# Layer 0's aggregation turned: weighted features stationary in 32-column groups, masked p moving, own waves for the denominators

## The chip, the cores and the metric

The kernel runs on one core of one Trainium2 chip. A core has a matrix engine (TensorE, PE in the profile, with its weight loads as PEld), a vector engine (VectorE, DVE), a scalar engine (ScalarE, ACT), a general engine (GpSimd, POOL) and an engine that here only starts transfers (SyncE, SP). Matrix products land in PSUM, eight banks of 128 partitions by 512 fp32 numbers; everything else works from on-chip memory. A product has a stationary operand, which is loaded as weights (up to 128 columns), and a moving operand that is streamed past it (up to 512 columns).

The metric is the device time of one execution in microseconds.

## The reference, cut to what matters

Thirty-two graphs of 512 nodes with 256 features go through four layers, each with a residual: a graph attention with 4 heads of 64 features (layer 0), one with one head and softmax over the other axis (1), one with scores from the features themselves (2), and a transformer block with 8 heads and a feed-forward part (3). The change is in layer 0:

```python
h = maximum(layernorm(x), 0)
Wh = (h @ W).reshape(B, N, H, F)                      # H = 4, F = 64
e_src = einsum('bnhf,hf->bnh', Wh, a_src)
e_dst = einsum('bjhf,hf->bjh', Wh, a_dst)
e = leaky_relu(e_src[:, :, None, :] + e_dst[:, None, :, :], 0.2)
e = where((A > 0)[..., None], e, -1e9)
alpha = softmax(e, axis=2)
Hout = elu(einsum('bijh,bjhf->bihf', alpha, Wh))
x = x + Hout.reshape(B, N, H * F)
```

For node i and head h, the sum over neighbours j of exp(e) times the features of j is wanted, and the sum of exp(e) itself, the denominator, to divide by.

## The kernel before, in words

All work is recorded first and put in order afterwards. `layer0` to `layer3` (lines 804 to 1061) call helpers of a `Plan`: `plan.dve`, `plan.act`, `plan.dma`, `plan.matmuls` (lines 220 to 273). Each call becomes a job of one engine. A job's place in the order is a number from a written list: `PLACES` (line 291) for the graphs in the middle and `OWN` (line 334) for the first three and the last three, one number per job in the order of recording, plus 100000 per graph. `carry_out` (line 179) sorts all jobs by place and issues them so; within an engine the order is fixed. The durations given in the calls (such as 0.867) were for whoever made the lists and do not act at run time. Because all instructions are issued from these helpers, the profile names lines 215, 236, 266 and 268 for nearly all of them, and one goes by the names of tiles. Four graphs are under way at a time: while layer 0 of graph b runs, so do layer 1 of b-1, layer 2 of b-2 and layer 3 of earlier ones. `WARM` (line 591) lists places at which products with no use are put in to keep TensorE going.

Tiles come from a few kinds of buffers (lines 623 to 633). `half` has 8 slots of 128x512 that `p`, `y`, `to` and `inv` share. `ps` has 8 slots, one for each PSUM bank. A job that needs a slot waits until the slot's last user is done.

Layer 0 of one graph: the normalised rows h are transposed and multiplied with the weights (`ps_wh`). With leaky ReLU of slope 0.2, exp(e_src + e_dst) is, up to a factor that the division by the denominator takes away, max of two products, so a tile of p needs one VectorE instruction: for head hd and block j of 128 source nodes, `p` = max(rows[hd], a column of rt) times the mask, 128 source nodes by 512 target nodes. `rows` has the target side's values spread over all partitions: a small transpose (`ps_sp`), a store to DRAM and a broadcast load (`spread`, line 750). `wh[:, j, hd]` has the 64 features of block j for head hd, weighted, and their weight as a 65th column, so one product gives both sums.

The aggregation before: head by head, four p tiles, then for each of four target blocks i four products that add up over j, each with a 128x128 piece of p stationary and the 65 columns of `wh` moving. The result for a head lies in one bank with target nodes on partitions; VectorE takes the reciprocal of column 64 and multiplies.

Layer 3 already has a step of the form that the change brings to layer 0. Its context product `ps_ct` has 32 columns of `v` stationary and p moving, four heads in one call, each in its own 32 partitions of the bank; `ps_to` sums the denominators in the same way with a block of ones. The chain behind `ps_to` is: copy to on-chip memory (`to`), a store and a load that reorder it (`seen`), a reciprocal (`turned`), a store and a broadcast load (`inv`), and the multiplication of `cT`. Then come the output projection `ps_wo`, a normalisation to `n`, its transposition to `tT` and the feed-forward products `ps_f`.

Of the kernel before, what the change touches and what calls it, by code (L numbers as in the profile page):

```python
# [19 lines left out]
P = 128  # L20
# [255 lines left out]
def cut(i, n):  # L276
    return slice(i * n, (i + 1) * n)
# [6 lines left out]
def width(args):  # L284
# [7 lines left out]
    22162, 0, 22162, 88531, 22162, 26725, 27163, 44460, 126207, 331647, 206240, 126207, 317201, 18267, 20761,  # L292
    18708, 20761, 20761, 20761, 19602, 20856, 20856, 20856, 21830, 21830, 21830, 22732, 23337, 26934, 26317,
    22732, 26696, 27107, 27107, 30449, 53386, 34079, 34079, 38928, 51388, 52104, 54992, 57816, 58763, 57816,
    60568, 60081, 64657, 58365, 58866, 58866, 60717, 59413, 60717, 69440, 61691, 69039, 58515, 59806, 61012,
    69310, 73463, 76565, 74335, 77480, 55624, 59714, 61810, 60113, 66193, 63085, 62613, 62147, 61810, 61828,
    66013, 71581, 76689, 73222, 74340, 71581, 80778, 81737, 82695, 84674, 95332, 99599, 91796, 94089, 94085,
    93641, 99780, 99871, 99871, 99871, 104897, 111173, 100627, 103661, 102330, 106673, 110040, 110040, 110439,
    110702, 110702, 111173, 103192, 98821, 100354, 103331, 104973, 109811, 109811, 114440, 115166, 117019,
    120459, 121784, 121784, 139316, 133372, 142407, 137472, 142753, 142177, 142576, 137500, 142780, 142780,  # L300
    142996, 142996, 145490, 146534, 182835, 158676, 172770, 165625, 182835, 182835, 184170, 184170, 185322,
    184815, 184929, 184929, 184929, 187876, 187397, 200306, 200306, 185322, 188856, 198107, 188211, 188638,
    192607, 197637, 197826, 198409, 201283, 201244, 200306, 208481, 210062, 211700, 211941, 233602, 234284,
    235911, 235911, 211941, 217912, 218005, 241001, 224079, 224079, 230987, 230987, 236039, 237560, 237560,
    241953, 245593, 248489, 249477, 249813, 250667, 250344, 253110, 255044, 255044, 255614, 260717, 250695,
    250667, 257382, 257239, 257910, 257011, 257816, 257582, 257910, 258536, 259626, 259626, 260717, 260717,
    262805, 263575, 263165, 265205, 264400, 265625, 266248, 266260, 266977, 265939, 265939, 265939, 266047,
    266654, 268571, 268656, 269410, 270114, 271651, 274286, 274286, 280210, 280492, 283576, 283576, 275998,
    270461, 272338, 272338, 272770, 275869, 283576, 283576, 283576, 292056, 279418, 280186, 281828, 287241,
    293813, 295621, 299513, 293813, 280342, 280342, 285316, 280607, 292528, 292528, 285495, 301515, 301515,  # L310
    293861, 309042, 323663, 299920, 310909, 323056, 302045, 313927, 315695, 324108, 326725, 328805, 333540,
    335674, 330312, 335674, 333540, 335674, 335674, 335674, 335674, 335674, 335674, 337792, 335674, 335945,
    337538, 337792, 338472, 338472, 339430, 338064, 338995, 339085, 339805, 339430, 341861, 340079, 342248,
    342386, 343136, 363657, 365495, 365712, 343496, 344786, 346786, 361418, 362306, 363732, 360543, 361672,
    363606, 363615, 364988, 366453, 366470, 366470, 367867, 371472, 350129, 350129, 351023, 351522, 350129,
    352607, 373487, 352053, 355399, 354213, 353318, 352495, 358682, 375835, 360752, 354916, 357414, 356045,
    356979, 356501, 363165, 376453, 365438, 357934, 359672, 361968, 358915, 359382, 367305, 376453, 367305,
    373487, 376011, 376011, 376214, 377681, 379922, 386609, 386609, 391610, 368361, 371551, 370334, 369094,
    370632, 372872, 389527, 372949, 376689, 376689, 376689, 375390, 376689, 389527, 379922, 378070, 379951,
    378381, 379951, 379951, 379951, 389752, 386116, 378530, 386611, 381015, 386341, 380335, 386655, 392660,  # L320
    386655, 391743, 393582, 393733, 397668, 393911, 397668, 398447, 399849, 404727, 406119, 396110, 408587,
    408587, 408587, 408587, 408532, 408672, 408672, 408672, 408672, 408833, 408587, 408672, 408672, 408901,
    409041, 408843, 408851, 409041, 409165, 409165, 409165, 409165, 409165, 409200, 409200, 412312, 412594,
    410533, 411146, 413463, 414091, 413863, 414031, 414685, 414779, 414604, 414779, 425712, 432774, 417564,
    417600, 418973, 414994, 418406, 418406, 417704, 420814, 423607, 416056, 423251, 424719, 419148, 419463,
    426062, 419047, 425810, 426096, 422579, 426020, 427996, 426052, 426052, 426481, 427471, 427663, 427663,
    428663, 428815, 428815, 428815, 428815, 428815, 428815, 428815, 436411, 441991, 442166, 442166, 442334,
    442892, 426062, 426062, 426062, 426062, 426062, 426120, 428517, 429214, 429626, 429626, 431772, 432297,
    432526, 438547, 440425, 440425, 440425, 445487, 442892, 445367, 445261, 445606, 444750, 445596, 445914,
    445914, 446041, 447300, 447300, 447822, 447822, 448286, 447822, 447822, 447822, 449213, 454171, 455710,  # L330
    501496, 619074, 561825,
# [4 lines left out]
        0, 0, 0, 119376, 103, 103, 103, 849, 849, 135780, 267957, 849, 12430, 0, 0, 0, 0, 0, 0, 0, 0, 0, 0, 0, 0, 0,  # L336
        0, 0, 0, 0, 0, 0, 0, 0, 0, 0, 0, 0, 0, 0, 0, 11, 11, 11, 11, 24105, 2715, 1981, 1981, 0, 11, 11, 12, 8848,
        13263, 12, 994, 0, 698, 698, 720, 24151, 18142, 11140, 30522, 698, 698, 698, 698, 698, 19312, 7058, 5132,
        698, 769, 769, 907, 12093, 907, 2071, 10598, 24151, 24151, 24427, 24427, 26204, 26204, 20723, 22597, 24775,
        17243, 24775, 24775, 24775, 26442, 29386, 30515, 24834, 27433, 27101, 27305, 27636, 28305, 28305, 28305,  # L340
        36756, 38640, 33391, 33391, 33391, 32763, 33391, 34992, 37365, 37365, 39631, 39631, 39631, 41962, 41990,
        44686, 43031, 46645, 46952, 48602, 50627, 50627, 50627, 50627, 52044, 52287, 52287, 52287, 54403, 57069,
        59970, 67793, 68704, 57330, 72067, 72067, 76307, 76307, 57069, 70179, 70179, 76449, 87103, 90440, 91113,
        91113, 86657, 91775, 91830, 89730, 89730, 89830, 84870, 88104, 88104, 91830, 95736, 146060, 95736, 110896,
        110896, 111056, 151052, 162807, 171370, 193307, 144090, 146060, 161198, 161281, 169706, 177493, 178851,
        193307, 159830, 168071, 175630, 192102, 193307, 194008, 203693, 203960, 204523, 208395, 211891, 211891,
        211891, 211891, 541, 206953, 207979, 217639, 217841, 208042, 220030, 219958, 222074, 223137, 223137, 223268,
        223695, 223695, 223695, 223695, 223962, 224666, 227528, 223695, 226442, 226476, 227561, 228090, 225042,
        226400, 226400, 227561, 227561, 229120, 243465, 241449, 251907, 251907, 251968, 261633, 261633, 261633,
        262685, 268778, 267860, 241176, 253160, 264725, 254084, 264725, 265569, 271684, 271711, 268778, 251945,  # L350
        258419, 272733, 270637, 272733, 281556, 281556, 274321, 266409, 266409, 272414, 268107, 274733, 275414,
        276199, 281751, 281751, 283148, 283148, 283148, 286088, 286088, 286088, 283645, 283645, 283645, 285852,
        283148, 286088, 283645, 285852, 283829, 286088, 287226, 287226, 287247, 287247, 287247, 290195, 290195,
        290195, 290324, 290324, 290927, 290324, 290324, 290324, 291288, 290195, 290380, 290783, 297351, 291438,
        311506, 407069, 309785, 314007, 314007, 352851, 353546, 353546, 320788, 320788, 320788, 328304, 334485,
        339755, 350640, 350991, 351191, 356570, 356636, 360260, 360260, 360260, 364578, 368069, 323179, 323676,
        323723, 323613, 323610, 356339, 367007, 324585, 327970, 329761, 330936, 330730, 345176, 372128, 358994,
# [231 lines left out]
}  # L589

WARM = [
    (1906, 1), (21908, 1), (24150, 2), (44209, 4), (45938, 1), (223694, 9),
]

def quick_path(
# [38 lines left out]
    def new(tag, name, shape, dtype=F32):  # L636
        return plan.tile(K[tag], name, shape, dtype)
# [958 lines left out]
```

## Time and profile before

| | us |
|---|---|
| median of 3 runs | 3472.92 |
| lowest and highest | 3470.82, 3476.01 |
| the profiled execution | 3479.19 |
| its span on the core | 3477.2 |
| TensorE busy | 3399.2 |
| VectorE busy | 2840.4 |
| ScalarE busy | 2082.5 |

The granted TensorE clock over the span was 0.993 of full speed. A row of the groups view names line and engine, the operation, the tiles written and read, the shapes and the count, then busy time and mean duration of one, then how long the engine stood idle before it and what ended that. A matrix product of fp32 operands appears as two passes with a weight load each; a transpose is one pass. Passes overlap in the pipeline, so a mean duration is longer than the distance from one start to the next; the rows in order of time give that distance.

### The profile page before, as it was taken

How to read it: one execution, taken by the hardware profiler on the slowest of the kernel's cores; microseconds unless marked ns; L12 is line 12 of the kernel's file. 1: busy time of each engine (PE TensorE's matmuls, PEld its weight loads, DVE VectorE, ACT ScalarE, POOL GpSimd, SP SyncE). 2: the span in 40 equal slices, each digit the busy share in tenths (PEclk: the TensorE clock that was granted, in tenths of full speed). 3: DMA queues.
4: the chain of work that ended last, by engine and by line, in shares of the span. 5: the costliest groups of instructions: out<-in, count | busy, mean ns of one | idle time of the engine just before them, and what ended most of it. 6: DMA issues, size and time to landing. Idle time of an engine off the chain costs nothing.

```text
span 3477.2 us, 49596 instructions
## 1 busy us (share of the span) xinstructions
PE 3399.2 (98%) x18474; PEld 2310.3 (66%) x18474; DVE 2840.4 (82%) x5659; ACT 2082.5 (60%) x4705; POOL 11.1 (0%) x25
## 2 busy tenths in 40 slices
PE   6999999999999999999999999999999999999996
PEld 5766766766666766666666666667667666667554
DVE  5888888888888788888888887888888888877874
ACT  4656566556576556675566665566665565764652
POOL 1000000000000000000000000000000000000000
PEclk9999999999999999999999999999999999999998
DMA  5111111111111111111111111111111120110000
GB/s 161 43 52 54 36 43 53 44 50 56 32 47 52 38 56 50 38 45 54 38 56 50 35 46 52 41 56 38 41 52 44 50 68 32 40 47 20 13 8 26
DMA packets 161176, 161.23 MB, mean 46 GB/s; under 512 B 92576, under 2 KB 126880, under 8 KB 156832
## 3 DMA queue, kind: packets, MB, share of 16 engines
q1 hardware_dynamic: 158464, 153.00, 14.8%
q0 software_dynamic: 1216, 3.94, 0.3%
q8 instruction: 147, 2.41, 0.3%
q10 hardware_dynamic: 1248, 1.05, 0.1%
q14 instruction: 101, 0.83, 0.1%
HBM read 122.96 MB, written 18.22 MB: 41 GB/s over the span
## 4 chain that ended last, share of the span: by engine, by line
PE 86%; DVE 7%; DMA 3%; ACT 2%; issue 1%; DVEq 0%; SPq 0%
PE ps_f L268 25%; PE ps_o L268 22%; PE ps_s L268 6%; PE ps_wh L268 6%; PE ps_ct L268 6%; PE ps_qk L268 5%; PE ps_t L266 4%; PE ps_e L268 4%; PE ps_wo L268 3%; DVE p L215 3%; PE ps_v L268 2%; DMA inv<-in_d 2%; DVE acc L215 2%; PE ps_to L268 1%; DVE st L215 1%
## 5 line engine op out<-in xcount | busy, mean ns | idle before, releaser
L268 PEld LDWEIGHTS ps_o<-wh,p 128*128 128x128 f32 x5120 | 673.1, 192 | 86.6 <-issue 55.0
L268 PE MATMUL ps_o<-wh,p 128*128 128x65 f32 (+1 forms) x5120 | 723.5, 295 | 0.4 <-DVE o L215 0.4
L215 ACT ACTIVATE p<-ps_s 128x512 f32<-128x512 f32 x1024 | 563.0, 625 | 59.9 <-PE ps_s L268 55.1
L215 DVE TENSOR_TENSOR p<-p,m 128x2048 f32<-128x2048 f32 x256 | 582.8, 2278 | 12.2 <-ACT p L215 12.0
L268 PE MATMUL ps_f<-ff_t,f 128*128 128x256 f32 x2048 | 476.4, 380 | 0.0
L268 PE MATMUL ps_f<-tT,ff_t 128*128 128x512 f32 x1024 | 454.4, 599 | 0.7 <-ACT tT L215 0.7
L268 PEld LDWEIGHTS ps_f<-ff_t,f 128*128 128x128 f32 x2048 | 377.9, 190 | 81.2 <-issue 34.0
L215 DVE SCALAR_TENSOR_TENSOR p<-rows,seen,mT 128x512 f32<-128x512 f32 x512 | 364.8, 740 | 14.6 <-PE ps_o L268 11.9
L268 PEld LDWEIGHTS ps_f<-tT,ff_t 128*128 128x128 f32 x1024 | 192.7, 191 | 229.8 <-issue 208.2
L215 ACT ACTIVATE h<-x,shift,rstd 128x256 f32<-128x256 f32 x512 | 299.2, 636 | 54.5 <-DVE shift L215 54.5
L215 ACT ACTIVATE rstd<-mv,eps 128x4 f32<-128x4 f32 x192 | 56.9, 297 | 446.8 <-DVE mv L215 262.0
L215 DVE TENSOR_TENSOR acc<-acc,p 128x2048 f32<-128x2048 f32 x128 | 292.9, 2288 | 3.2
L268 PE MATMUL ps_s<-qk 32*128 32x512 f32 x2048 | 287.6, 633 | 0.8 <-ACT qk L215 0.8
L268 PE MATMUL ps_qk<-h3T,wqkv_t 128*128 128x512 f32 x512 | 249.0, 594 | 1.2 <-ACT p L215 1.2
L268 PE MATMUL ps_o<-h,p 128*128 128x257 f32 x1024 | 246.7, 384 | 0.0
L268 PE MATMUL ps_ct<-p,v 128*32 128x512 f32 x2048 | 244.7, 595 | 1.4 <-ACT v L215 1.4
L215 ACT ACTIVATE f<-ps_f,ff1b_c 128x512 f32<-128x512 f32 x256 | 163.1, 682 | 125.9 <-PE ps_f L268 125.8
L268 PEld LDWEIGHTS ps_o<-h,p 128*128 128x128 f32 x1024 | 189.6, 190 | 47.1 <-PE ps_to L268 20.1
L266 PE MATMUL ps_t<-ident,h 128*128 128x128 f32 x1024 | 173.7, 278 | 29.2 <-ACT h L215 27.4
L215 DVE BATCH_NORM_STATS2 st<-x 128x6 f32<-128x256 f32 x512 | 196.5, 413 | 2.5 <-DMA x<-in_x_dram 0.6
L215 ACT COPY wh<-ps_wh 128x258 f32<-128x258 f32 x128 | 47.8, 377 | 239.5 <-PE ps_wh L268 236.7
L266 PEld LDWEIGHTS ps_t<-ident,h 128*128 128x128 f32 x1024 | 127.4, 144 | 82.7 <-issue 46.9
(126 smaller groups left out, 4600.9 us busy)
## 6 DMA issues: line engine op xcount, KB each, us to landing
adj<-in_adj_dram SPq DMA_DIRECT2D x32, 1024.0 KB
rows<-rows_d SPq DMA_DIRECT2D x32, 1024.0 KB
x<-in_x_dram SPq DMA_DIRECT2D x32, 512.0 KB
rows<-rows_d SPq DMA_DIRECT2D x32, 512.0 KB
inv<-in_d SPq DMA_DIRECT2D x64, 256.0 KB
out_dram<-y SPq DMA_DIRECT2D x32, 512.0 KB
mT<-m SPq DMA_TRANSPOSE x128
ff_t<-in_L_gnn_W_dram POOLq DMA_DIRECT2D x2, 1024.0 KB, 10.5
```

The costliest lines, as they stand in the source:

```text
L215: return [getattr(unit, method)(*map(real, args), **{k: real(v) for k, v in kw.items()})]
L266: made.append(self.nc.tensor.transpose(*map(real, c)))
L268: made.append(self.nc.tensor.matmul(*map(real, c[:3]), start=c[3], stop=c[4]))
```

## The change

The products of layer 0's aggregation are turned around. The stationary operand is now 32 columns of the weighted features, and the moving operand is a whole p tile of 512 target nodes. Two heads with two halves of 32 features each fill the four 32-column groups of the array, and their sums the four 32-partition groups of one bank; two such banks (`ps_oT`) hold the 256 features. A third bank (`ps_den`) holds the denominators: per head the weight column, repeated 32 times, is stationary. All three add up over the four source blocks, so the loop now goes over j outside and heads inside. At the end the sums have features on partitions: ScalarE copies each bank to a `half` tile (`oT`), four transposes each bring it back (`ps_or`), and VectorE takes one reciprocal for all heads and multiplies two heads at a time. The lists `PLACES`, `OWN` and `WARM` are new throughout, so the order of all other work is changed too; only `WARM` is shown.

```diff
 WARM = [
-    (1906, 1), (21908, 1), (24150, 2), (44209, 4), (45938, 1), (223694, 9),
+    (6839, 2), (6909, 5), (32585, 1), (47866, 3), (152849, 1), (210837, 9), (342049, 1),
 ]
...
         inv = rt[:, 2 * H0 :]
-        for hd in range(H0):
+        pairs, half = H0 // 2, F0 // 2
+        ps_oT = [new("ps", "ps_oT", [P, N]) for _ in range(pairs)]
+        ps_den = new("ps", "ps_den", [P, N])
+        for j in range(NT):
             ps_t = []
-            for j in range(NT):
+            for hd in range(H0):
                 p = new("p", "p0", [P, N])
                 plan.dve(
                     "scalar_tensor_tensor", p, rows[:, hd], rt[:, H0 + hd, j : j + 1], mT[:, j], OP.max, OP.mult,
                     fixed=0.21,
                 )
                 ps_t.append(p)
-            ps = new("ps", "ps_o", [P, NT, F0 + 1])
+            for g in range(pairs):
+                plan.matmuls(
+                    0.882,
+                    *(
+                        (
+                            ps_oT[g][cut(q, half)], wh[:, j, 2 * g + q // 2, cut(q % 2, half)], ps_t[2 * g + q // 2],
+                            j == 0, j == NT - 1,
+                        )
+                        for q in range(4)
+                    ),
+                )
+            plan.matmuls(
+                0.882,
+                *(
+                    (
+                        ps_den[cut(hd, half)], wh[:, j, hd, F0 : F0 + 1].flat(lambda t: t.to_broadcast([P, half])),
+                        ps_t[hd], j == 0, j == NT - 1,
+                    )
+                    for hd in range(H0)
+                ),
+            )
+        turned = []
+        for ps in (ps_den, *ps_oT):
+            t = new("half", "oT", [P, N])
+            plan.act("copy", t, ps)
+            ps = new("ps", "ps_or", [P, NT, P])
             for i in range(NT):
-                plan.matmuls(
-                    0.867,
-                    *((ps[:, i], ps_t[j][:, cut(i, P)], wh[:, j, hd], j == 0, j == NT - 1) for j in range(NT)),
-                )
-            plan.dve("reciprocal", inv[:, hd], ps[:, :, F0], each=7.5e-3, fixed=0.13)
+                plan.matmuls(0.11, (ps[:, i], t[:, cut(i, P)], ident))
+            turned.append(ps)
+        plan.dve(
+            "reciprocal", inv.flat(lambda t: t.rearrange("p h t -> p t h")),
+            turned[0][:, :, 0:P:half], each=7.5e-3, fixed=0.13,
+        )
+        for g in range(pairs):
             plan.dve(
-                "tensor_mul", o[:, :, cut(hd, F0)], ps[:, :, :F0],
-                inv[:, hd].flat(lambda t: t.unsqueeze(2).to_broadcast([P, NT, F0])),
+                "tensor_mul", o[:, :, cut(g, P)].split("p t (h f) -> p t h f", (NT, 2, F0), h=2),
+                turned[1 + g].split("p t (h f) -> p t h f", (NT, 2, F0), h=2),
+                inv[:, 2 * g : 2 * g + 2].flat(
+                    lambda t: t.rearrange("p h t -> p t h").unsqueeze(3).to_broadcast([P, NT, 2, F0])
+                ),
             )
```

## The prediction

> **What bounds the kernel now.** I read the engine rows of the page first, then the chain, then the groups by form, and last the order of time on TensorE inside one graph of the steady middle.
>
> ```profile
> PE 3399.2 (98%) x18474; PEld 2310.3 (66%) x18474; DVE 2840.4 (82%) x5659; ACT 2082.5 (60%) x4705; POOL 11.1 (0%) x25
> ...
> PEclk9999999999999999999999999999999999999998
> ...
> PE 86%; DVE 7%; DMA 3%; ACT 2%; issue 1%; DVEq 0%; SPq 0%
> ```
>
> TensorE works 98% of the span at full clock and is 86% of the chain that ended last. A busy PE row need not be a PE at its peak, so what one product costs has to be read from start to start. Groups by form (busy us and mean ns, then idle before):
>
> ```profile
> L268 PEld LDWEIGHTS ps_o<-wh,p 128*128 128x128 f32 x5120 | 673.1, 192 | 86.6 <-issue 55.0 <-ACT wh L215 1.1 <-DVE y L215 0.8
> L268 PE MATMUL ps_o<-wh,p 128*128 128x65 f32 x4096 | 481.8, 273 | 0.0
> L268 PE MATMUL ps_ct<-p,v 128*32 128x512 f32 x2048 | 244.7, 595 | 1.4 <-ACT v L215 1.4
> L215 ACT COPY cT<-ps_ct 128x512 f32<-128x512 f32 x64 | 37.3, 587 | 16.8 <-PE ps_ct L268 16.7
> L215 DVE RECIPROCAL seen<-ps_o 128x4 f32<-128x4 f32 x128 | 22.0, 172 | 49.5 <-PE ps_o L268 49.3
> ```
>
> The second row is what the change takes out: 2048 products, two passes each, moving only 65 columns against 128 stationary ones. The third row, layer 3's context product, already has the new form: 32 stationary columns, 512 moving, four such products side by side (a wave of eight passes). Order of time on TensorE in one graph, and around one lone wave earlier on (start, length, x passes):
>
> ```profile
> 1774.51 1.91 PE L268 MATMUL ps_wh<-w_t,h1T 128*128 128x258 f32 x8
> 1776.34 2.78 PE L268 MATMUL ps_ct<-p,v 128*32 128x512 f32 x24
> 1778.94 1.04 PE L268 MATMUL ps_to<-acc,ones 128*32 128x512 f32 x8
> 1779.80 1.04 PE L268 MATMUL ps_ct<-p,v 128*32 128x512 f32 x8
> 1780.77 2.01 PE L268 MATMUL ps_o<-h,p 128*128 128x257 f32 x8
> ...
> 1784.03 3.68 PE L268 MATMUL ps_o<-wh,p 128*128 128x65 f32 x32
> 1787.55 1.96 PE L268 MATMUL ps_o<-h,p 128*128 128x257 f32 x8
> ...
> 1792.46 3.19 PE L268 MATMUL ps_wo<-wo_t,cT 128*128 128x256 f32 x14
> 1795.49 0.78 PE L268 MATMUL ps_o<-wh,p 128*128 128x65 f32 x6
> ```
> ```profile
> 387.47 1.06 PE L268 MATMUL ps_to<-acc,ones 128*32 128x512 f32 x8
> 388.47 1.14 PE L268 MATMUL ps_s<-qk 32*128 32x512 f32 x8
> ```
>
> There are no gaps: each line starts as the one before releases the array. A 65-column pass takes (1787.55-1784.03)/32 = 0.110 us, more than a quarter of what a 512-column one takes. Five waves in a row take 1780.77-1776.34 = 4.43 us and a lone one 1.00, so a further wave costs (4.43-1.00)/4 = 0.857. Entering and leaving the four-column mode costs 1.00-0.857 = 0.14 inside the run, and 0.10 on the product ahead of it: eight passes of ps_wh take 1.83 where 0.216 each (14 passes of ps_wo in 3.03) make 1.73. So 0.24 us per run of waves.
>
> **The change on TensorE.** It is the engine that sets the end, so every term counts in full.
> - Out: 4096 passes x 0.110 = 450.6.
> - In: per graph 4 source tiles x 3 waves (two of weighted features, one of denominators) = 12, times 32 = 384 waves x 0.857 = 329.1.
> - In: 3 x 4 transposes per graph, 384. Seven transposes start at 1751.57 and the next product at 1752.33, so 0.109 each: 41.9.
> - In: mode changes. In the planned order of the two programs, column-mode runs rise from 75 to 138, because most of the new waves stand in two runs of six per graph: 63 x 0.24 = 15.1. Row-mode runs (ps_s) go from 223 to 221, nothing.
> - In: warming products 18 to 22, eight passes more: 1.7.
>
> In is 387.8, out 450.6: **-62.8 us** with no new wait.
>
> Two features of the new waves the trace does not show. Two column groups of a weighted-feature wave stream the *same* p tile, where layer 3's four stream four tiles; and the denominator's stationary columns are one column repeated. Between the free end (0.857, as ps_ct) and full serialisation of the pair (two turns, 1.71, on 256 waves: +219), I take the ps_ct row, as it is the same shape from the same kind of memory. A repeated column can at most make its weight load longer; loads lie under the 0.43 us of the pass before.
>
> Here the Trainium skill speaks against the change. "TensorE: Matmul & The Clock Gate", Part 3, gives 2.38 for three column tiles, not 3; at the same 79% four tiles would give 3.17, and a wave, 4 x 0.857 unpacked (512 columns, two passes of 0.43), would be 1.08 us: 384 x 0.22 = 86 more, and the change would lose 23. "TensorEngine Tiling (Array Packing)", Key Properties, adds that changing the mode drains the array. The trace has both at their price here: 0.857 per wave, 0.24 per run. I sum with the rows.
>
> **The change elsewhere.** VectorE loses 128 reciprocals x 0.172 and 128 products of 256 x 0.413 (74.9 us) and gains 32 reciprocals of 16 x 0.247 and 64 products of 512 x 0.686 (51.8): 0.7 us less per graph. The 16 masked p tiles per graph stay. ScalarE gains 96 copies of 128x512 at 0.587: 56 us, 1.8 per graph, on an engine that is busy 64.9 of the 104.7 us that a graph takes in the middle of the run (from 1747.90 to 1852.60, one row spread of layer 0 to the next). These are covered by TensorE's work except at two places.
>
> (1) *Feed-forward entry.* The out-projection's sums go through VectorE's statistics, four normalisations and tT on ScalarE before ps_f may start. In the graph above ps_wo ends at 1795.49 and ps_f starts at 1802.53: 7.04 us, covered by 65-column products and transposes. After, the planned order covers it with a six-wave run (5.38), eight transposes of n (0.87) and eight of the turned sums (0.87): 7.1, just enough. But two of the new copies (1.17 us) stand on ScalarE's queue between n and tT; what is late next is tT, then ps_f. ScalarE waited 0.42 for its transposes at that point, so up to 0.75 is exposed, down to nothing where the copies fit into such holes.
>
> (2) *The second cT.* VectorE's queue from layer 3's first mask product to this multiplication is full. The trace has it so:
>
> ```profile
> 1787.75 2.75 DVE L215 SCALAR_TENSOR_TENSOR p<-rows,seen,mT 128x512 f32<-128x512 f32 x4 [0.27 <-PE ps_o L268]
> 1791.60 0.69 DVE L215 TENSOR_TENSOR cT<-cT,inv 128x512 f32<-128x512 f32 x1 [1.10 <-DMA inv<-in_d]
> ```
>
> cT ends at 1792.29 and ps_wo starts at 1792.46: no slack already. Summing the rows' durations along VectorE's queue to that point gives 56.0 us in both orders (14 p tiles now stand ahead of it, 12 before, against small work moved out), and TensorE's order gives 57 us in both. So the wait stays as it is, within some 0.5 per graph. Each wave also needs four heads of one source tile; eight p tiles feed a six-wave run and the pool of that size holds eight, shared with y, to and inv. p tiles cost 0.74 each, 3.0 per three waves of 2.57: they must be ahead when a run begins, and the other products between the two runs (some 5 us) let them be.
>
> On SP the number of transfers is unchanged; the layer-0 rows load now follows the first inv load instead of preceding the pair, and has some 9 us before its first use, as 7.5 passed in the trace from its issue at 1750.37 to the first p at 1757.90. I price it at nothing; late rows would delay the first run of waves one for one.
>
> I take 0.45 us per graph for (1) and (2) together, over 29 graphs (the first three fill the pipeline): +13. Sum: -62.8 + 13 = **-50**. The profiled execution took 3479.2 (span 3477.2), which becomes 3429; the median of the runs, 3472.9, becomes **3423**.
>
> **Rivals.**
> - *All covered* (chance 0.15). Waits stay as they are; 3472.9-62.8 = 3410, and about 3395 if the 78 us in which TensorE is not busy (3477.2-3399.2, nearly all in the first and last slices of the page) shrink as well. For it: steady graphs idle little. Against: the copies ahead of tT.
> - *Evacuation and VectorE set the pace* (0.17). Three sums stay in PSUM from the first wave to the last and leave together, ScalarE copies before tT, and a late cT adds to it: 1.5 to 2 us per graph, 44 to 58 of the 62.8 come back: 3454 to 3468, at the worst end no change. For it: VectorE busy 57.94 of the 60 us from 1735 to 1795. Against: the queue sums of (2) are equal.
> - *The waves are dearer than ps_ct's* (0.08), the slower side. If the two groups that stream one p tile take turns, up to +219: 3473-50+219 = 3642. It decides from 50/384 = 0.13 us per wave. For it: no row has that form. Against: four streams run side by side in ps_ct at no cost over one.
> - *The order is not kept in runs*, or array time per graph is otherwise as before (0.02): 3473.
>
> **How the numbers follow.** The case of the sum has 0.58, with its own range 3408 to 3445. A measurement of this kernel tells 0.2% (7 us) from no change: the runs span 5 us. Faster: 0.58 + 0.15 + 0.13 of the pace rival = 0.86. Same: 0.03 of it + 0.02 = 0.05. Slower: 0.08 + 0.01 = 0.09. The range reaches from part of the covered case, 3394, to most of the pace rival, 3460.
>
> **What would show it.** ps_oT and ps_den passes, 3072 in all, with runs of six waves taking 0.14 + 6 x 0.857 = 5.28 us; 384 ps_or passes at 0.109; a steady graph, 104.7 now, at about 103.1; VectorE busy 20 lower, ScalarE 56 higher. Step (1) shows as idle time of ps_or or ps_f waiting for oT or tT. The prediction is wrong if a wave takes over 0.98 us, or if ps_wo or the first wave of a run waits over 1 us per graph.

## The result, and the profile after

The changed kernel takes 3427.1 us (median of four runs, 3424.9 to 3429.9) against 3473.7 for the kernel before on the same chip: a ratio of 0.9867, 95% interval 0.9850 to 0.9884. The forecast was 3423, in a range of 3394 to 3460. Its profiled execution took 3424.9, with a span of 3422.9.

The engine rows, the granted clock and the chain that ended last, from the page of the changed kernel:

```profile
PE 3340.2 (98%) x17842; PEld 1975.5 (58%) x17842; DVE 2820.1 (82%) x5499; ACT 2115.6 (62%) x4801; POOL 11.1 (0%) x25
...
PEclk9999999999999999999999999999999999999997
...
PE 85%; DVE 8%; DMA 4%; ACT 3%; issue 1%; DVEq 0%; SPq 0%; ACTq 0%
```

TensorE's busy time fell by 59.0 us, from 3399.2, and the time in which it isn't busy rose from 3477.2-3399.2 = 78.0 to 3422.9-3340.2 = 82.7: together the 54.3 us by which the two spans differ. (The medians differ by 46.6, since the profiled execution of before lay 5.5 above its median and that of after 2.2 below.) The groups by form (busy us and mean ns, then idle time before and what ended it):

```profile
L268 PE MATMUL ps_ct<-p,v 128*32 128x512 f32 x2048 | 247.8, 599 | 0.0
...
L268 PE MATMUL ps_oT<-p,wh 128*32 128x512 f32 x2048 | 240.6, 594 | 0.0
...
L268 PE MATMUL ps_den<-p,wh 128*32 128x512 f32 x1024 | 129.5, 597 | 0.0
...
L268 PEld LDWEIGHTS ps_oT<-p,wh 128*32 128x32 f32 x2048 | 64.3, 110 | 142.4 <-issue 128.3 <-DVE st L215 8.3 <-DVE p L215 2.3
...
L266 PE MATMUL ps_or<-ident,oT 128*128 128x128 f32 x384 | 62.4, 273 | 0.1
...
L215 ACT COPY oT<-ps_oT 128x512 f32<-128x512 f32 x64 | 37.0, 580 | 14.0 <-PE ps_oT L268 14.0
...
L215 DVE RECIPROCAL seen<-ps_or 128x16 f32<-128x16 f32 x32 | 8.0, 251 | 5.5 <-PE ps_or L266 5.5
```

The 3072 passes of `ps_oT` and `ps_den` take what those of `ps_ct` take (594 and 597 ns against 599, overlapped), a weight load of 32 columns is 110 ns long where that of 128 was 192, and the 384 transposes hardly wait. The repeated column of the denominators costs nothing at its load either: 110 ns at the median, as for the others. One reciprocal of 16 per partition and graph takes the place of four. Order of time on TensorE in a graph of the steady middle (start, length, x passes, and in brackets the wait):

```profile
1635.38 1.06 PE L268 MATMUL ps_to<-acc,ones 128*32 128x512 f32 x8
...
1642.33 1.06 PE L268 MATMUL ps_den<-p,wh 128*32 128x512 f32 x8
1643.21 2.76 PE L268 MATMUL ps_oT<-p,wh 128*32 128x512 f32 x24
1645.79 1.06 PE L268 MATMUL ps_den<-p,wh 128*32 128x512 f32 x8
1646.67 1.04 PE L268 MATMUL ps_oT<-p,wh 128*32 128x512 f32 x8
1647.64 2.00 PE L268 MATMUL ps_o<-h,p 128*128 128x257 f32 x8
1649.49 0.59 PE L268 MATMUL ps_wo<-wo_t,cT 128*128 128x256 f32 x2
1650.64 2.86 PE L268 MATMUL ps_wo<-wo_t,cT 128*128 128x256 f32 x12 [0.56 <-DVE cT L215]
1653.43 3.64 PE L268 MATMUL ps_oT<-p,wh 128*32 128x512 f32 x32
1656.89 1.90 PE L268 MATMUL ps_den<-p,wh 128*32 128x512 f32 x16
1658.72 1.13 PE L266 MATMUL ps_t<-ident,n 128*128 128x128 f32 x8
1659.68 1.04 PE L266 MATMUL ps_or<-ident,oT 128*128 128x128 f32 x8
...
1660.70 1.98 PE L268 MATMUL ps_f<-tT,ff_t 128*128 128x512 f32 x4
```

The second run of six waves lasts from 1653.43 to 1658.72, 5.29 us; the forecast had 5.28. The first, 1642.33 to 1647.64, takes 5.31. A wave that streams one p tile into two column groups, and one whose weights are a single column repeated, cost what `ps_ct`'s cost: 5.29 less the 0.14 at the start is 0.858 for each of six. In this stretch TensorE waits once, 0.56 us for the second cT.

Over the 23 graphs between the row spreads of graphs 5 and 28, start to start, a graph takes 103.41 us (105.29 before). The 64 narrow products took 14.1 us of it before; the twelve waves take 10.6 and the twelve transposes 1.3. The order of all other work is new as well, and the old form in a newly made order was not run. But in these 23 graphs TensorE stood idle for 8.9 us in all before and for 5.4 after, so a better order alone had little to win there.

### The profile page after: what moved, and what is told of

It reads as the page before. It is cut to its first block, busy times and chain, and to the rows that moved or that the text cites. A ratio compares the mean times of both kernels' runs of the same rounds, so it can differ in the third digit from the quotient of the medians.

```text
span 3422.9 us, 48320 instructions
## 1 busy us (share of the span) xinstructions
PE 3340.2 (98%) x17842; PEld 1975.5 (58%) x17842; DVE 2820.1 (82%) x5499; ACT 2115.6 (62%) x4801; POOL 11.1 (0%) x25
## 4 chain that ended last, share of the span: by engine, by line
PE 85%; DVE 8%; DMA 4%; ACT 3%; issue 1%; DVEq 0%; SPq 0%; ACTq 0%
PE ps_f L268 25%; PE ps_o L268 11%; PE ps_s L268 7%; PE ps_qk L268 6%; PE ps_wh L268 5%; PE ps_ct L268 5%; PE ps_oT L268 5%; PE ps_t L266 4%; PE ps_e L268 4%; PE ps_wo L268 3%; DVE p L215 3%; PE ps_v L268 3%; PE ps_den L268 3%; DMA inv<-in_d 2%; DVE acc L215 2%; PE ps_to L268 1%
## 5 line engine op out<-in xcount | busy, mean ns | idle before, releaser
L215 ACT ACTIVATE p<-ps_s 128x512 f32<-128x512 f32 x1024 | 555.3, 616 | 35.0 <-PE ps_s L268 33.7
L268 PE MATMUL ps_f<-tT,ff_t 128*128 128x512 f32 x1024 | 467.1, 597 | 0.4 <-ACT tT L215 0.4
L215 DVE SCALAR_TENSOR_TENSOR p<-rows,seen,mT 128x512 f32<-128x512 f32 x512 | 352.7, 744 | 32.6 <-PE ps_oT L268 20.6
L215 ACT ACTIVATE h<-x,shift,rstd 128x256 f32<-128x256 f32 x512 | 283.1, 599 | 94.5 <-DVE shift L215 94.2
L268 PEld LDWEIGHTS ps_f<-tT,ff_t 128*128 128x128 f32 x1024 | 185.4, 191 | 196.2 <-issue 154.5
L268 PE MATMUL ps_o<-wh,p 128*128 128x256 f32 x1024 | 242.9, 385 | 0.4 <-ACT wh L215 0.4
L268 PE MATMUL ps_oT<-p,wh 128*32 128x512 f32 x2048 | 240.6, 594 | 0.0
L268 PE MATMUL ps_qk<-h3T,wqkv_t 128*128 128x512 f32 x512 | 239.2, 599 | 0.0
L268 PEld LDWEIGHTS ps_o<-wh,p 128*128 128x128 f32 x1024 | 189.9, 190 | 77.0 <-issue 25.9
## 6 DMA issues: line engine op xcount, KB each, us to landing
ff_t<-in_L_gnn_W_dram POOLq DMA_DIRECT2D x2, 1024.0 KB, 10.3
```

The costliest lines, as they stand in the source:

```text
L215: return [getattr(unit, method)(*map(real, args), **{k: real(v) for k, v in kw.items()})]
L268: made.append(self.nc.tensor.matmul(*map(real, c[:3]), start=c[3], stop=c[4]))
```

## The experiments

All times are medians beside the 3427.1 of the changed kernel, which was timed with the result alone; the kernel before took 3472.8 to 3475.3 beside the experiments and 3473.7 beside the changed kernel, so differences of 2 or 3 us say nothing. "Per graph" is the mean over the same 23 graphs, and a product's share of it is counted from each pass's start to the next one's. The letters in the expectations, in short: A, TensorE's list alone sets the end; B, the new order is needed for the gain; C, VectorE sets the pace; D, a change of the array's mode costs less than priced; E, a product's price goes with its moving columns; F, TensorE's and VectorE's lists are equally long; G, a chain of waits runs beside TensorE's list.

**The new form in the old order.** The turned products stand where the old ones stood, with the tables of before; a job is put off only where no buffer is free.

```diff
-PLACES = [ ... ]                      # of after
+PLACES = turned_places(PLACES)        # of before: p tiles and waves at the old places,
+OWN = {n: turned_places(t) for n, t in OWN.items()}   # copies, transposes, products after the last wave
...
-        for number, j in enumerate(sorted(self.jobs, key=lambda j: j.place)):
+        for number, j in enumerate(self.in_turn()):
```

> The turned aggregation in the written order of the kernel before: the new products, copies and transposes stand at the places of the old ones, and a job is put off only where no buffer is free; all other work keeps its place. Theory A (the array time of the aggregation is the gain, whatever the order): TensorE's list loses 450.6 us of 65-column passes and gains 384 waves x 0.857 = 329.1, 384 transposes x 0.109 = 41.9 and, as the waves now stand in 201 runs instead of 138, (201-75) x 0.24 = 30.2: -49, so 3425, and up to 3440 with waits for copies that nothing hides. Theory B (the new written order brings the gain, the form alone does not): 3465 or more.

Measured: 3683.5 us (3681.3 to 3686.6), ratio to before 1.0609 [1.0591, 1.0627]. A graph takes 112.7 us. The products' own time is about 102 of it, as in the changed kernel, but waits make up some 10 us (TensorE is idle for 6.5 by the profile), against about 1.5 in the kernels before and after. TensorE's waits in this kernel (who for whom on which engine: us in total, times, longest):

```profile
PE ps_wh L307 <- DVE p L254: 48.5, 25, 3.0
PE ps_t L305 <- DVE p L254: 47.1, 52, 1.4
...
PE ps_f L307 <- ACT tT L254: 21.4, 32, 1.5
PE ps_wo L307 <- DVE t L254: 18.8, 24, 0.8
```

The products of the first two rows don't read p. The view of the tile `ps_y` (layer 2's transposes) tells what they wait for; among those who waited for an instruction that uses it are (us, times):

```profile
  PE ps_wh L307: 48.5, 25
  PE ps_t L305: 47.1, 52
```

These are the same waits: each ends when VectorE has read `ps_y` out of its PSUM bank into a tile p, so the product waits for a bank. Of the eight banks three are now held from the first wave of a graph to the last, where the old form held one per head. In the changed kernel neither waits for `ps_y`. That the banks make up the whole of the waits wasn't measured. The form alone doesn't bring the gain; it needs an order that fits it. One placement was tried, which needn't be the best.

**Fewer waves.** One denominator wave per graph in place of four.

```diff
+            if j:
+                plan.at += 1
+                continue
             plan.matmuls(0.882, ... ps_den ...
-                        ps_t[hd], j == 0, j == NT - 1,
+                        ps_t[hd], True, True,
```

> The kernel after with the denominator waves of three of the four source blocks left out (so the denominators are partial): 96 waves fewer, all other engines unchanged. Theory A (TensorE still bounds every graph): 96 x 0.857 = 82 less than the kernel after, 3345. Theory C (VectorE's queue of p tiles and masks sets the pace once TensorE is faster): half or less of it, 3385 or more.

Measured: 3432.0 (3427.5 to 3435.9). 96 waves are gone, 82 us of TensorE's list, and nothing is gained: a graph takes 103.90. The same stretch of this kernel, in order of time on TensorE:

```profile
1650.47 2.86 PE L268 MATMUL ps_wo<-wo_t,cT 128*128 128x256 f32 x12 [1.77 <-DVE cT L215]
1653.26 3.64 PE L268 MATMUL ps_oT<-p,wh 128*32 128x512 f32 x32
1657.93 0.82 PE L266 MATMUL ps_t<-ident,n 128*128 128x128 f32 x3 [1.03 <-ACT n L215]
1658.91 0.76 PE L266 MATMUL ps_t<-ident,n 128*128 128x128 f32 x5 [0.16 <-ACT n L215]
```

What was work has become waiting: for cT, which needs the attention's denominators back from DRAM, and for n, the layer norm behind it. The chain that ended last is 70% TensorE here (85% in the changed kernel), with VectorE 17% and DMA 6%.

**More waves.** Each denominator wave is done twice.

```diff
+                    for turn in (0, 1)
                     for hd in range(H0)
```

> The kernel after with every denominator wave issued twice (the denominators are doubled): 128 waves more, nothing else. Theories A and F: each wave lies on TensorE's path, 128 x 0.857 = +110 on the kernel after, 3537, and per graph 103.35 becomes 106.8. A smaller step, under +70, would mean that TensorE has hidden slack.

Measured: 3521.5 (3518.6 to 3524.9), 94 more for 128 waves: 0.74 each, and 106.54 per graph, 3.13 more for four waves (0.78 each). The four waves themselves take 3.46 us from start to start, 0.86 each; `ps_wo` takes 0.31 less, as part of the new work replaces its wait for cT. So TensorE's list does set the end, and has no room to shrink below it: up costs nearly in full, down gives nothing.

**More changes of the mode.** A full-array transpose stands ahead of the first source block's waves, into the same bank.

```diff
+                    *([(ps_oT[g][:, :P], ident, ident)] if j == 0 else []),
```

> The kernel after with one plain full-array transposition ahead of each of the three waves of a graph's first source block (96 in all; what they write is overwritten by the wave). Runs of waves rise from 138 to 199. Theory A (entering and leaving the four-column mode costs 0.24 us): 96 x 0.109 + 61 x 0.24 = +25, so 3452. Theory D (the mode change costs nothing, only the transpositions count): +10, 3437.

Measured: 3445.2 (3442.4 to 3448.3), 18 more, between the two theories (25 and 10); per graph 0.72 more. Three transposes are 0.33 of that, so two further runs cost 0.39, 0.20 each. On TensorE of this kernel:

```profile
1649.49 0.27 PE L266 MATMUL ps_den<-ident 128*128 128x128 f32 x1
1649.69 1.07 PE L268 MATMUL ps_den<-p,wh 128*32 128x512 f32 x8
1650.69 0.33 PE L266 MATMUL ps_oT<-ident 128*128 128x128 f32 x1
1650.95 1.07 PE L268 MATMUL ps_oT<-p,wh 128*32 128x512 f32 x8
1651.94 0.33 PE L266 MATMUL ps_oT<-ident 128*128 128x128 f32 x1
```

A transpose and a lone wave take 1.20 and 1.25 us here; less 0.109 and 0.857, the change of mode costs 0.23 and 0.28, as the forecast's 0.24. The graph pays less because `ps_wo` takes 0.21 less in this kernel: again work replaces its wait for cT.

**The old form with half the columns.** The kernel before, with 33 moving columns in place of 65, so that half of the features are left out.

```diff
-(ps[:, i], ps_t[j][:, cut(i, P)], wh[:, j, hd], j == 0, j == NT - 1)
+(ps[:, i, 32:], ps_t[j][:, cut(i, P)], wh[:, j, hd, 32:], j == 0, j == NT - 1)
```

> The kernel before with 33 instead of 65 moving columns in layer 0's aggregation (half of the features are left out, and the other half stands in their place). Theory A (such a pass is bound by loading its 128 stationary columns): a pass stays at 0.110 us and the time at 3474 within 7. Theory E (it is bound by what it streams): passes fall to 0.06 us or less, 4096 x 0.05 = 205 less, about 3270.

Measured: 3628.3 (3616.6 to 3633.9), ratio 1.0446. The median pass still takes 0.112 us, start to start, so the price of the old form was not in its moving columns. What both have in common is a load of 128 stationary columns ahead of each pass; that the load sets the price is the reading that is left, not one shown apart. The rest of the time is a surprise, told at the end.

**VectorE relieved.** Layer 3's sums of p for the denominators take two source blocks of four (four additions of 2.28 us fewer per graph); once on the changed kernel, once on the one with fewer waves.

```diff
                 if j == 0:
                     first_p = p
+                elif j > 1:
+                    plan.at += 1
                 else:
```

> The kernel after with layer 3's denominators taken from two of the four source blocks: VectorE's queue is 9.1 us per graph shorter, TensorE's list is unchanged. Theory F: TensorE bounds the graph as well, so 3427 within 10. Theory C (VectorE's queue alone sets the pace): some 9 per graph less, down to TensorE's own waits, 3390 or below.

> The kernel after with three of four denominator waves of layer 0 left out, as in the run before, and with layer 3's denominators taken from two of the four source blocks, which leaves four additions of 2.28 us per graph out of VectorE's queue ahead of the second cT (9.1 us per graph; both sets of denominators are partial). Theory F (TensorE's list and VectorE's queue were equally long per graph, so that shortening one alone gave nothing): the 82 us of waves now come out in full, about 3345. Theory G (what held the run before back is the round trip of layer 3's denominators through DRAM, or ScalarE): no more than 10 below it, 3420 to 3435.

Measured: 3418.5 (3417.4 to 3423.5) and 3419.5 (3416.0 to 3425.5). Nine microseconds of VectorE per graph buy 8.6 us in all, and in the middle a graph takes 103.34 instead of 103.41. So VectorE's total work isn't the pace (C had 3390 for the first), nor are two equally long lists enough to explain why leaving out waves gave nothing (F had 3345 for the second).

**ScalarE's copies twice.** Each of the three copies of sums is made twice over.

```diff
-            plan.act("copy", t, ps)
+            plan.put("ACT", 1.2, 1.3, [t], [ps],
+                lambda t=t, ps=ps: [nc.scalar.copy(t.real(), ps.real()) for _ in range(2)])
```

> The kernel after with each of the three copies out of PSUM made twice: 96 more copies, 56 us more on ScalarE, of which one pair per graph stands ahead of tT. If step (1) of the prediction holds (copies ahead of tT are exposed by up to 0.75 us per graph), doubling them exposes 1.17 more per graph: +34, 3461. If they lie under TensorE's work, as the trace after suggests: 3427 within 10.

Measured: 3471.2 (3464.8 to 3477.9), 44 more; a graph takes 105.12, 1.71 more. On TensorE of this kernel:

```profile
1685.73 1.13 PE L266 MATMUL ps_t<-ident,n 128*128 128x128 f32 x8
1687.17 0.66 PE L266 MATMUL ps_or<-ident,oT 128*128 128x128 f32 x4 [0.32 <-ACT oT L863]
1688.28 0.66 PE L266 MATMUL ps_or<-ident,oT 128*128 128x128 f32 x4 [0.45 <-ACT oT L863]
```

The copies come out above all ahead of `ps_or`, which stands ahead of `ps_f`: 1.2 of the 1.71 us. They are free once and not a second time.

**The trip through DRAM taken away.** Layer 3's reciprocal denominators are made on ScalarE straight from `ps_to`, as exp(-ln x); the first half of the trip stays for the guard at the end. Once on the changed kernel, once on the one with fewer waves.

```diff
+            plan.put("ACT", 1.2, 1.3, [inv], [ps_to], lambda inv=inv, ps_to=ps_to: (
+                nc.scalar.activation(inv.real(), ps_to.real(), AF.Ln),
+                nc.scalar.activation(inv.real(), inv.real(), AF.Exp, scale=-1.0)))
...
-            plan.dve("reciprocal", turned, part, each=7.5e-3, fixed=0.13)
-            plan.dma(d2 ... turned, 0.05)
-            plan.dma(inv, d2 ... 2.9)
```

> The changed kernel with the attention's reciprocal denominators (inv of layer 3) made on ScalarE straight from ps_to, as exp of minus ln, instead of by the trip through DRAM and back (to, to_d, seen, reciprocal, in_d, inv); the first half of that trip stays, since the final guard reads it. Theory G (in the steady graphs the stretch from the last ps_to to the first ps_f of the feed-forward is as long as a chain of waits that runs beside TensorE's list: denominators through DRAM, cT, ps_wo, layer norm, n, tT; in the changed kernel list and chain are equal within half a microsecond, 24.2 us): the wait of ps_wo for cT (0.3 to 0.5 us per graph) goes, no more, so -5 to -15 us, 3412 to 3422. Rival (ScalarE is the engine at its edge, so two more activations of 0.6 us per half cost time): 3430 to 3450.

> The same edit on the kernel that leaves out three of the four denominator waves of layer 0 (3432 us measured, with waits of 1.2 us for cT ahead of ps_wo and 1.2 us for n ahead of ps_t in every graph). Theory G: the trip was ps_wo's wait; without it cT's multiplication is bound by its place in VectorE's queue, 1.1 us earlier, so -1.1 us in each of 29 graphs, about 3400 (3388 to 3410); the wait of ps_t for n stays, since only the four waves of ps_oT lie between ps_wo and it. If the trip isn't on the second chain: 3425 to 3440.

Measured: 3425.3 (3424.1 to 3426.0), no difference and in neither of the expected ranges; and 3420.2 (3418.6 to 3422.1), 12 less where 32 was expected. The wait for cT did go: `ps_wo` takes 3.55 us of a graph in place of 3.93, and on the kernel with fewer waves 4.34 in place of 5.03. But `ps_s` takes 0.65 and 0.64 more. The trip is on a second chain; ScalarE, where I put its work, is on another one.

**Fewer waves elsewhere.** The changed kernel without three of four `ps_ct` waves in the first half of layer 3's heads: again 96 waves, outside the stretch from the last `ps_to` to the first `ps_f`.

```diff
+                if g == 0 and j:
+                    plan.at += 1
+                else:
                     plan.matmuls(0.882, ... ps_ct ... j == 0, g == 0 or j == NT - 1)
```

> The changed kernel without three of the four ps_ct waves of the first half of layer 3's heads (so the output of layer 3 is not that of the reference): 96 waves fewer, as many as in the run that left the denominator waves out, but outside the stretch between the last ps_to and the first ps_f. Theory G (outside that stretch, 79 us of each graph's 103, TensorE's own list sets the time; all runs so far have 72.1 us from ps_f to the next row spread whatever was edited): the 96 waves of 0.857 us come off whole, -82 us, 3345 (3340 to 3360). Rival (a second chain as long as TensorE's list everywhere, VectorE's or ScalarE's queue): no gain, 3420 to 3435, as in the run that left out denominator waves.

Measured: 3426.9 (3425.5 to 3428.4): no gain, and theory G, with its one stretch, falls. A graph takes 103.61. ScalarE of this kernel at the place where the waves were:

```profile
1718.27 0.63 ACT L215 ACTIVATE p<-ps_s 128x512 f32<-128x512 f32 x1
1718.75 0.62 ACT L215 ACTIVATE y<-ps_e,nshift 128x384 f32<-128x384 f32 x1
1719.21 2.11 ACT L215 ACTIVATE p<-ps_s 128x512 f32<-128x512 f32 x4
1721.12 1.25 ACT L215 ACTIVATE y<-ps_e,nshift 128x512 f32<-128x512 f32 x2
```

and, of TensorE's waits over the run:

```profile
PE ps_to L268 <- ACT p L215: 15.3, 24, 0.6
PE ps_wh L268 <- DVE spr L215: 5.5, 24, 0.3
```

ScalarE works without a gap from 1713.6 to 1722.4, mostly on exponentials, and `ps_to` now waits for them 24 times. The excess of `ps_s` (1.2 us per graph), `ps_ct` with `ps_to` (0.9) and `ps_wh` (0.5) over the changed kernel makes up the 2.6 that the waves left. So the steady graph has at least two places, the way into the feed-forward and layer 3's scores, where something other than TensorE is about as long as TensorE's list.

**The trip taken away where ScalarE has room.** The same edit for the second half of the heads alone, whose `ps_to` comes after the exponentials.

```diff
+            if g:
+                ...                      # exp(-ln) on ScalarE, as above
+            else:
+                ...                      # the trip through DRAM, as in the changed kernel
```

> The changed kernel with the reciprocal made on ScalarE for the second half of layer 3's heads alone; the first half keeps its trip through DRAM. With both halves on ScalarE ps_wo's wait for cT went (0.33 us per graph) but a wait of ps_s of 0.53 came, where ScalarE is full of exponentials. If each of the two belongs to its own stretch: ps_wo's wait goes, ps_s keeps its time, so -0.33 us in each of 29 graphs, -8 to -10 us, about 3417 (3413 to 3421). If ScalarE's work is priced wherever it is put: 3424 to 3430, no gain.

Measured: **3408.6** (3407.5 to 3409.9), ratio to before 0.9816 [0.9803, 0.9830]: 18.5 less than the changed kernel, twice what was expected, and faster than both kernels, with the whole of the work done. The chain that ended last, from its page:

```profile
PE 94%; DVE 3%; ACT 2%; DMA 1%; issue 1%; ACTq 0%; SPq 0%; DVEq 0%
```

`ps_wo`'s wait is gone and `ps_s` is as it was; a graph takes 103.16. That is 5.7 us over the 23 graphs. Filling the pipeline (to graph 5) takes 4.3 less and the stretch from graph 31's row spread to the end 6.6 less. Of these 10.9 us TensorE's idle time makes up 7.0, which fits a trip that is covered less where fewer graphs are at work beside each other, though that wasn't tested. The other 3.9 are busy time of the same number of passes, and the granted clock was higher there (1.00 against 0.99, and 0.96 against 0.95): that part of the surplus need not be the edit's.

## Why the prediction was right, step by step

*The array's term.* -62.8 was worked out. TensorE's busy time fell by 59.0; a run of six takes 5.29 (5.28), a transpose 0.109 (0.109), a change of mode 0.23 and 0.28 (0.24). It held because each duration was read from start to start of a row of the same shape. The forecast's estimate from the Trainium skill's 2.38 for three column tiles ("TensorE: Matmul & The Clock Gate", Part 3) would have made a wave 1.08 and the change a loss of 23; the traces have 0.857 for the old waves and 0.858 for the new ones, and the measurement decides. "The waves are dearer" is refuted by the 5.29.

*Step (1), two copies ahead of tT.* The forecast allowed up to 0.75 us per graph. ScalarE in the changed kernel, at the same graph:

```profile
1656.95 2.08 ACT L215 ACTIVATE n<-t,shift,rstd 128x256 f32<-128x256 f32 x4 [0.72 <-DVE shift L215]
1658.93 0.56 ACT L215 COPY oT<-ps_den 128x512 f32<-128x512 f32 x1
1659.40 0.58 ACT L215 COPY oT<-ps_oT 128x512 f32<-128x512 f32 x1
1659.87 1.44 ACT L215 ACTIVATE tT<-ps_t,b_c,g_c 128x512 f32<-128x512 f32 x2
```

The two copies take 0.94 from start to start, while TensorE transposes n (0.96, from 1658.72 to 1659.68). tT couldn't have started sooner. The forecast took the hole in ScalarE as 0.42 from the profile before; the new order made it as long as the copies. Exposed: nothing; `ps_f` waits for tT 0.4 us in the whole run. Doubling them put tT 4.16 us after the start of n instead of 2.92 and cost 1.71 per graph, so the place was named rightly and the cover is gone at once. ScalarE's busy time rose by 33 and not by 56. The same lines show a part of the reason: back to back, a copy of 0.58 takes 0.47, which makes 45 for 96; the rest stays open.

*Step (2), the second cT.* In the changed kernel, on VectorE:

```profile
1648.97 0.16 DVE L215 RECIPROCAL seen<-ps_o 128x1 f32<-128x1 f32 x1
1649.90 0.69 DVE L215 TENSOR_TENSOR cT<-cT,inv 128x512 f32<-128x512 f32 x1 [0.77 <-DMA inv<-in_d]
```

The queue reaches cT in time and waits for inv, as before. Over the run VectorE waited there 24.1 us (39.7 before) and `ps_wo` 15.6 (16.8): unchanged, as the sums of the queue had said. What the step missed is that this wait could be removed: in the kernel of the last experiment `ps_wo` waits for cT 1.7 us over the whole run.

*The waits' sum.* 0.45 us per graph was put on top for both places, and in the steady graphs it didn't come: counted from start to start, their waits are about 1.5 us per graph before and after, and the middle 23 graphs gave 43.1 of the 45.1 that the sum has for them. A graph went from 105.29 to 103.41 us; the forecast's 104.7 was that of a single graph. That the +13 was right in size all the same (62.8-46.6 = 16 by the medians, 8.5 by the profiled pair) was luck: in the profiled pair 2.0 are lost in the middle and the other 6.5 while the pipeline fills and drains. Filling to graph 5 took 10.3 us longer, 8.7 of it busy time of TensorE, as the new order does more of the later layers before that point (160 passes of `ps_ct` where there were 128). The stretch from graph 28 to the end took 21.5 less; there TensorE is idle for 41.5 us, where it was 34.9. The other 8 us between pair and medians can't be placed, as there is one trace of each.

*The rivals.* "All covered" came true in the steady middle and missed by the ends. "Evacuation and VectorE set the pace" is refuted for VectorE by its relief (8.6 us for 9 us in each graph), but its other half, three sums held in PSUM, is real where the order isn't made for it (3683, with 95.6 us of waits for the bank of `ps_y` alone). The forecast took the new order as a given cover and didn't price the banks. "Order not kept in runs": it was kept, the 138 column-mode runs of the planned order are in the trace, 54 of them of six waves.

## What to carry to other kernels

Price a turned product from start to start of a row that has its shape, and count its runs; here that gave the fall of TensorE's busy time within 4 us. Before hoping for more from the same place, take work out and put work in: where adding costs in full and taking out gives nothing, other chains are as long as the engine's list, and the next gain lies in the waits (here up to 18.5 us for one trip through DRAM, and only where the engine that takes over the work has room). A form that holds its accumulators longer may need an order of its own: here the old one cost 256 us more.

## What was not expected of the hardware

The kernel with 33 moving columns was slower than the one with 65 though nothing waited for anything new. The stretches of its run around one burst of narrow products (bounds, length, busy time with the number of instructions of TensorE, its weight loads, VectorE, ScalarE and GpSimd, then the granted clock, the share of the DMA engines and GB/s):

```profile
1765.00:1770.00 5.00, 5.00 (x38) 4.74 (x37) 4.38 (x15) 0.50 (x2) 0.00 (x0) 1.00 0.00 0
1770.00:1775.00 5.00, 5.00 (x28) 5.00 (x28) 1.46 (x9) 2.08 (x4) 0.00 (x0) 0.55 0.38 84
1775.00:1780.00 5.00, 5.00 (x17) 3.45 (x16) 3.36 (x12) 1.55 (x2) 0.00 (x0) 0.50 0.72 232
1780.00:1785.00 5.00, 5.00 (x12) 2.10 (x11) 1.24 (x8) 0.65 (x2) 0.00 (x0) 0.93 0.00 0
```

and TensorE at their beginning:

```profile
1767.07 5.44 PE L268 MATMUL ps_o<-wh,p 128*128 128x33 f32 x40
```

Some 31 narrow passes into this burst of 40, at 1770.5, the granted clock falls to one half, with the busy row full throughout (5.00 of 5.00), and stays there for some 10 us, so that the wide products behind pay for it. A burst of 32 such passes at 1755.62 had left it at 1.00. Over the span the clock was at half for 373 us (52 before, 43 in the changed kernel), its mean 0.949, and a graph took 109.4 us. The Trainium skill ("TensorE: Matmul & The Clock Gate", Part 1) has the clock halved after a window in which the array is idle; here it wasn't idle by the profile, but a pass of 0.112 us moved only 33 columns, some 28 ns at the 0.43 us that 512 columns take. That the clock goes by the columns moved is argued from this one kernel, not shown. With 65 columns, 40 such passes in a row (from 1795.49 in the kernel before) leave the clock at 1.00.
